# State-space layer and feed-forward on one core: where the sums over a chunk come from

## The chip, the cores and the metric

The kernel runs on one core of a Trainium2 chip. A core has five engines with queues of their own: TensorE (PE; its weight loads are listed as PEld), VectorE (DVE), ScalarE (ACT), GpSimd (POOL) and SyncE (SP), which here issues DMA transfers. The metric is the device time of one execution in microseconds; a comparison uses the median of several runs.

## The reference

For 16 sequences of 512 tokens with 256 channels, x goes through two blocks with a residual each. The first is a state-space layer (8 heads of 64, state size 128); the second a feed-forward layer with ternary weights. What matters here is the scan of the first:

```
dt = softplus(dt + dt_bias);  A = -exp(A_log)
dA = exp(dt * A)                      # per token and head
S  = dA_t * S + xdt_t B_t             # state, token after token
y_t = S C_t
```

With a = dt * A, a product of dA over a range of tokens is the exponential of a sum of a over that range.

## The kernel before

A sequence is cut into NC = 4 chunks of P = 128 tokens, and the scan is done chunk by chunk with matrix products. For each sequence and each of its 32 pairs (chunk, head), W = NC * NH, the kernel needs four things made of sums of `a`:

- the running sum at each token, as rows (`cum`, 32 x 128) and, transposed, as columns (`cums`, 128 x 32);
- the rows broadcast to all 128 partitions: `cum` is written to DRAM (`raw`, L464) and read back once for each chunk as `mt` (128 x 8 x 128, `stage_r`, L518). Then `relu(cums - mt)` is taken head by head (`stage_s`, L545, ScalarE; for the first sequence's chunks 1 to 3 `stage_s_v`, L532, VectorE), and an exponential over the tile (`stage_b1`, L556): the decay between two tokens of a chunk;
- `ecum`, the exponential of the rows (L485), broadcast through DRAM as `ct` (L495) and multiplied on POOL (L506);
- `dec` (L480): the exponential of two sums, the one over the tokens after each token of its chunk (`dec[:, 0]`) and the one over the whole chunk (`dec[:, 1]`). POOL uses the first in `xend` (L610), which feeds the product `pst` (L630) that updates the state, and the second to decay the state (L658).

`sums_of` makes all of them with products on TensorE: `after` and `ones` times `a` (L456) for the two sums of `dec`, copied by VectorE to `sums` (L462); `a` times `incl` (L457) for the rows, copied by ScalarE to `cum` (L461); and a transpose of `cum` (L468), copied to `cums` (L470). An f32 product of two operands is two passes on TensorE, each with its weight load.

Around this stand, for each sequence b: `stage_a` (projections `pm` L300 and `pz` L322, the causal convolution `cv` on ScalarE L305 and VectorE L307, silu L312 and L326, `dt` through `dtr` L339 and the transpose `pqt` L344), `stage_a2` (softplus, ends with `a`, L442), `stage_b2` (the chunks: transposes `px` L595, `pg` L601 and L602, `pst`, `py` L644 and L651, then `y` L663, `zs` L667, L574, L575), `stage_c1` (output projection `po` L716, norms, transposes of x3 and its split `x3p` L745 to L750) and `stage_c2` (feed-forward: `ph` L762, `hT` L768, `pf` L796). `stage_a0` and `stage_t0` give x (L259) and its transpose (`pt_a` L277, copied to `x1T` L280).

The order on each of the four compute engines is the order of issue in the program, which `interleave` makes: each stage is a generator with a sum of work and a place (from, to) between 0 and 1, and the stage whose next step has the smallest place goes on. After a prologue for sequences 0 and 1, the loop over i = 1 to 14 has two parts in a turn. The first part runs the projections of sequence i + 1 beside the output projection of i - 1; the second the chunks of i and the feed-forward of i - 1, beside the decays of i + 1. In the turn i = 1 the decays of sequence 1 are still done in the first part. Every wait is in order: an instruction that waits holds up all that is behind it on its engine.

Of the kernel before, what the change touches and what calls it, by code (L numbers as in the profile page):

```python
# [28 lines left out]
F32 = mybir.dt.float32  # L29
BF16 = mybir.dt.bfloat16  # L30
AF = mybir.ActivationFunctionType
ALU = mybir.AluOpType
# [3 lines left out]
P = 128  # L36
# [5 lines left out]
NH = 8  # L42
# [18 lines left out]
def mamba_ffn_kernel(  # L61
# [35 lines left out]
    def load_x(b):  # L97
# [12 lines left out]
    nc.gpsimd.affine_select(  # L110
        out=incl, in_=ones, compare_op=ALU.is_ge, fill=0.0, base=0,
        pattern=[[1, P]], channel_multiplier=-1,
    )
    after = const.tile([P, P], F32)
    nc.gpsimd.affine_select(
        out=after, in_=ones, compare_op=ALU.is_gt, fill=0.0, base=0,
        pattern=[[-1, P]], channel_multiplier=1,
    )
    mhalf = const.tile([P, NC], F32)
    nc.gpsimd.memset(mhalf, -0.5)  # L120
# [327 lines left out]
    def sums_of(b):  # L448


        W = NC * NH
        a = seqs[b].pop("a")
        af = a.rearrange("p c h -> p (c h)")
        pd = ps_tr.tile([P, 512], F32, tag="tr", name=f"pd_{b}")
        for i, tri in enumerate((after, ones)):
            nc.tensor.matmul(pd[:, i * W : (i + 1) * W], tri, af, start=True, stop=True)  # L456
        nc.tensor.matmul(pd[0:W, 2 * W : 2 * W + P], af, incl, start=True, stop=True)  # L457
        sums = small.tile([P, 2, W], F32, tag="sums", name=f"sums_{b}")
        pc = pd[0:W, 2 * W : 2 * W + P]
        cum = small.tile([W, P], F32, tag="cum", name=f"cum_{b}", bufs=1)  # L460
        nc.scalar.copy(cum, pc)  # L461
        nc.vector.tensor_copy(sums.rearrange("p i w -> p (i w)"), pd[:, 0 : 2 * W])  # L462
        raw = dram.tile([W, P], F32, tag="raw", name=f"raw_{b}")
        nc.sync.dma_start(raw, cum)  # L464
        seqs[b].update(sums=sums, cum=cum, raw=raw)
        yield 0.15
        turned = pd[:, 2 * W + P : 3 * W + P]
        nc.tensor.transpose(turned, cum, ident[0:W, 0:W])  # L468
        cums = small.tile([P, W], F32, tag="cums", name=f"cums_{b}", bufs=2)
        nc.vector.tensor_copy(cums, turned)  # L470
        seqs[b].update(cums=cums)
        yield 0.15


    def stage_b0(b):


        s = seqs[b]
        s["dec"] = small.tile([P, 2, NC, NH], F32, tag="dec", name=f"dec_{b}")
        nc.scalar.activation(  # L480
            s["dec"].rearrange("p i c h -> p (i c h)"), s["sums"].rearrange("p i w -> p (i w)"),
            AF.Exp,
        )
        ecum = small.tile([NC * NH, P], F32, tag="ecum", name=f"ecum_{b}", bufs=1)
        nc.scalar.activation(ecum, s.pop("cum"), AF.Exp)  # L485
        s["way"] = dram.tile([NC * NH, P], F32, tag="way", name=f"way_{b}")
        nc.sync.dma_start(s["way"], ecum)
        yield 0.1

    def stage_d(b):  # L490
# [35 lines left out]
    def stage_s_v(b, *chunks):  # L526

        s = seqs[b]
        for c in chunks:
            mt = s["mts"][c]  # L530
            for h in range(NH):
                nc.vector.tensor_scalar(  # L532
                    mt[:, h, :], mt[:, h, :], s["cums"][:, c * NH + h : c * NH + h + 1], 0.0,
                    ALU.subtract, ALU.min,
                )
                if h % 2 == 1:
                    yield 0.25

    def stage_s(b, *chunks):

        s = seqs[b]
        for c in chunks:
            mt = s["mts"][c]
            for h in range(NH):
                nc.scalar.activation(  # L545
                    mt[:, h, :], mt[:, h, :], AF.Relu,
                    bias=s["cums"][:, c * NH + h : c * NH + h + 1], scale=-1.0,
                )
                if h % 2 == 1:
                    yield 0.25  # L550
# [266 lines left out]
    def chain(*stages):  # L817
        for st in stages:
            yield from st
# [39 lines left out]
    with tc.manual_schedule(engines=ordered):  # L859
        interleave(  # L860
            (
                chain(stage_a0(0), stage_t0(0), stage_a(0, FIRST, 2)),
                A0_WORK + T0_WORK + A_WORK, 0.0, 1.0,
            ),
            (stage_a0(1), A0_WORK, 0.04, 0.28),
            (chain(stage_sil(0), stage_a2(0, False)), 0.8, 0.42, 0.64),
            (sums_of(0), 0.3, 0.78, 0.86),
            (stage_r(0, 0, 1, 2, 3), 0.4, 0.865, 0.88),
            (scales(1), 3.0, 0.55, 0.8),
        )  # L870
        run(stage_t0(1))
        run(stage_a6(0))
        interleave(
            (stage_a(1, SECOND, 2), A_WORK, 0.0, 0.8),
            (stage_s_v(0, 1, 2, 3), 3.0, 0.03, 0.18),
            (stage_s(0, 0), 1.0, 0.182, 0.184),
            (chain(stage_b0(0), stage_d(0), stage_b1(0, 0)), 0.3, 0.185, 0.187),
            (stage_b1(0, 1, 2, 3, sign=1.0), 0.3, 0.22, 0.225),
            (stage_b2(0), B2_WORK, 0.2, 0.88),
            (chain(stage_sil(1), stage_a2(1, False)), 0.8, 0.28, 0.44),  # L880
            (sums_of(1), 0.3, 0.5, 0.56),
            (ternary(1), 4.0, 0.52, 0.54),
            (stage_e(0), E_WORK, 0.27, 0.52),
            (scales(2), 3.0, 0.3, 0.6),
            (stage_r(1, 0), 0.1, 0.57, 0.571),
            (stage_r(1, 1), 0.1, 0.58, 0.581),
            (stage_a0(2), A0_WORK, 0.5, 0.75),
            (stage_s(1, 0), 1.0, 0.7, 0.74),
            (stage_s(1, 1), 1.0, 0.76, 0.79),
            (stage_r(1, 2), 0.1, 0.66, 0.661),  # L890
            (stage_r(1, 3), 0.1, 0.82, 0.821),
            (stage_t0(2), T0_WORK, 0.81, 0.83),
            (stage_a6(1), 0.1, 0.84, 0.841),
            (ternary(2, 0, 2), 2.0, 0.9, 0.91),
        )
        for i in range(1, NB - 1):
            interleave(
                (ending(), 0.1, 0.0, 0.01),
                *([(ternary(2, 2, 4), 2.0, 0.02, 0.08)] if i == 1 else []),
                *([(stage_a6(i), 0.1, 0.12, 0.13)] if i > 1 else []),  # L900
                (stage_a(i + 1, BESIDE, 2), A_WORK - 1.72, 0.0, 1.0),
                (
                    chain(
                        stage_b0(1), stage_d(1), stage_b1(1, 0, 1), stage_s(1, 2), stage_b1(1, 2),
                        stage_s(1, 3), stage_b1(1, 3),
                    ),
                    2.6, 0.015, 0.2,
                )
                if i == 1
                else (chain(stage_s(i, 3), stage_b1(i, 3)), 1.1, 0.0, 0.01),  # L910
                (stage_c1(i - 1), C1_WORK, 0.0, 1.0),
                (stage_e(i), E_WORK, 0.32, 1.0),
            )
            run(stage_a1(i + 1))
            second = [
                (stage_r(i + 1, 0, 1), 0.2, 0.365, 0.37),
                (stage_s(i + 1, 0), 1.0, 0.44, 0.49),
                (stage_b0(i + 1), 0.1, 0.5, 0.51),
                (stage_b1(i + 1, 0), 0.1, 0.515, 0.52),
                (stage_s(i + 1, 1), 1.0, 0.53, 0.61),  # L920
                (stage_b1(i + 1, 1), 0.1, 0.62, 0.63),
                (stage_r(i + 1, 2), 0.1, 0.63, 0.64),
                (stage_s(i + 1, 2), 1.0, 0.72, 0.8),
                (stage_b1(i + 1, 2), 0.1, 0.81, 0.82),
                (stage_r(i + 1, 3), 0.1, 0.82, 0.83),
            ]
            second.append((stage_c2(i - 1), C2_WORK, 0.02, 1.0))
            second.append((stage_b2(i), B2_WORK, 0.0, 0.98))
            second.append((stage_a2(i + 1), A2_WORK, 0.08, 0.36))
            second.append((stage_a5(i + 1), 1.7, 0.58, 0.66))  # L930
            second.append((stage_d(i + 1), 0.1, 0.92, 0.93))
            if i + 2 < NB:
                second.append((stage_a0(i + 2), A0_WORK, 0.6, 0.9))
                second.append((stage_t0(i + 2), T0_WORK, 0.94, 0.97))
            interleave(*second)
        run(stage_s(NB - 1, 3))
        run(stage_b1(NB - 1, 3))
        run(stage_a6(NB - 1))
        interleave(
            (ending(), 0.1, 0.0, 0.01),  # L940
            (stage_c1(NB - 2), C1_WORK, 0.0, 0.235),
            (stage_e(NB - 1), E_WORK, 0.03, 0.16),
            (stage_b2(NB - 1), B2_WORK, -0.02, 0.4),
            (stage_c2(NB - 2), C2_WORK, 0.235, 0.98),
            (stage_c1(NB - 1), C1_WORK, 0.42, 0.9),
        )
        interleave((ending(), 0.1, 0.05, 0.06), (stage_c2(NB - 1), C2_WORK, 0.0, 1.0))
# [43 lines left out]
```

## Time and profile before

| what | us |
|---|---|
| median of 3 runs | 1138.25 |
| the runs | 1136.69, 1138.25, 1140.64 |
| the profiled execution | 1138.89 |
| its span, first to last instruction | 1137.2 |
| one turn of the loop, `pst` of a sequence to that of the next | 67.20 |
| L456, four passes, on the chain that ended last | 0.37 |
| `dec` (L480), mean of 16 | 0.256 |
| sums copy (L462), mean of 16 | 0.218 |
| relu of one head (L545), mean of 488 | 0.388 |

How to read the profile: every engine's rows are of one execution. The busy share says how full an engine is, the chain of waits which work the end of the run waited for: it is followed back from the last instruction, at each step to what released it or to the instruction before it on its engine. In a timeline a row holds the start and the length in us, the engine, the line, the operation, `out<-in` with shapes and the count of merged instructions; in brackets the idle time before it and what ended it. Successive instructions of an engine may overlap at their ends.

### The profile page before, as it was taken

What the parts mean: (1) busy time and instruction counts of PE and PEld (TensorE: products, weight loads), DVE (VectorE), ACT (ScalarE), POOL (GpSimd) and SP (SyncE); (2) the same over time, 40 slices, a digit from 0 to 9 for tenths busy, and PEclk for the clock granted to TensorE, in tenths of its full rate; (3) what the DMA queues carried; (4) which work ended last, traced back from release to release, by engine and by line L of the source; (5) the groups of instructions that cost most, each with busy time, mean ns of one, the idle gap of its engine ahead of it and who ended that gap; (6) DMA issues with size and microseconds to landing.
All of it is one profiled execution on the core that took longest, in us unless ns stands there. A gap on an engine that the chain in (4) does not pass through costs nothing.

```text
span 1137.2 us, 17164 instructions
## 1 busy us (share of the span) xinstructions
PE 1076.8 (95%) x6052; PEld 708.8 (62%) x6052; DVE 826.9 (73%) x2141; ACT 696.4 (61%) x1378; POOL 581.9 (51%) x695
## 2 busy tenths in 40 slices
PE   5777999999999999999999999999999999999797
PEld 2334475665757567575766757576574756657575
DVE  4797859677695867769686786967778596776552
ACT  4738667566756665676666567666666675665421
POOL 1243646355464635646464565635446463556742
PEclk9998999999999999999999999999999999999899
DMA  5221130221203121220311212022120302212000
GB/s 200 107 97 59 32 128 28 77 93 57 95 20 134 34 76 75 76 94 19 124 46 57 94 56 103 29 90 79 57 94 27 133 29 76 74 57 94 1 10 28
DMA packets 34534, 81.23 MB, mean 71 GB/s; under 512 B 4368, under 2 KB 23440, under 8 KB 32400
## 3 DMA queue, kind: packets, MB, share of 16 engines
q1 hardware_dynamic: 32896, 79.97, 20.3%
q8 instruction: 48, 0.79, 0.3%
q10 hardware_dynamic: 1552, 0.16, 0.1%
q14 instruction: 38, 0.31, 0.1%
HBM read 71.21 MB, written 8.91 MB: 70 GB/s over the span
## 4 chain that ended last, share of the span: by engine, by line
PE 56%; POOL 17%; DVE 16%; ACT 8%; issue 2%; DMA 1%; POOLq 0%; ACTq 0%; DVEq 0%
PE pf L796 19%; PE ph L762 12%; POOL ct L506 9%; PE pm L300 6%; PE py L644 5%; ACT mt L545 4%; PE pst L630 4%; DVE cv L307 4%; PE py L651 3%; POOL x3p L750 3%; DVE st_f L228 2%; DVE x L702 2%; ACT cv L305 2%; ACT mt L556 1%; POOL xend L610 1%
## 5 line engine op out<-in xcount | busy, mean ns | idle before, releaser
L307 DVE SCALAR_TENSOR_TENSOR cv<-pm,cw_sb,cv 128x511 f32<-128x511 f32 (+2 forms) x288 | 215.3, 748 | 62.7 <-ACT cv L305 55.5
L796 PE MATMUL pf<-w_sb,hT 128*128 128x256 f32 x1024 | 238.0, 382 | 0.0
L796 PEld LDWEIGHTS pf<-w_sb,hT 128*128 128x128 f32 x1024 | 190.0, 190 | 35.8 <-issue 11.5
L762 PE MATMUL ph<-x3p,w_bf 128*128 128x512 bf16 x768 | 188.7, 380 | 4.3 <-POOL x3p L750 1.9
L300 PE MATMUL pm<-x1T,win_sb 128*128 128x512 f32 x384 | 186.5, 609 | 1.2 <-ACT state L633 0.9
L768 ACT ACTIVATE hT<-ph,b_sb 128x512 f32<-128x512 f32 x128 | 87.9, 688 | 130.1 <-PE ph L762 129.9
L545 ACT ACTIVATE mt<-mt,cums 128x128 f32<-128x128 f32 x488 | 152.3, 388 | 0.0
L667 POOL TENSOR_TENSOR zs<-y,zs 128x512 f32<-128x512 f32 x64 | 81.3, 1271 | 105.8 <-DVE y L663 104.2
L716 PE MATMUL po<-wo_sb,zs 128*128 128x256 f32 x512 | 123.5, 385 | 2.2 <-DVE att L722 2.1
L322 PE MATMUL pz<-x1T,win_sb 128*128 128x512 f32 x256 | 121.7, 598 | 3.7 <-DVE sp_a L431 3.7
L762 PEld LDWEIGHTS <-w_bf 128*128 128x128 bf16 x768 | 70.3, 98 | 87.9 <-issue 22.7
L300 PEld LDWEIGHTS pm<-x1T,win_sb 128*128 128x128 f32 x384 | 71.5, 194 | 72.5 <-issue 65.1
L506 POOL TENSOR_TENSOR ct<-ct,xbc 128x1024 f32<-128x1024 f32 x48 | 112.3, 2365 | 3.7 <-DMA ct<-way 3.7
L716 PEld LDWEIGHTS po<-wo_sb,zs 128*128 128x128 f32 x512 | 94.9, 190 | 29.9 <-issue 14.4
L305 ACT ACTIVATE cv<-pm,cw_sb 128x512 f32<-128x512 f32 x96 | 65.0, 677 | 70.4 <-PE pm L300 68.9
L575 POOL TENSOR_TENSOR y<-y 128x256 f32<-128x256 f32 x64 | 46.9, 733 | 115.6 <-ACT y L574 115.6
L663 DVE SCALAR_TENSOR_TENSOR y<-xbc,dsk,py 128x128 f32<-128x128 f32 x256 | 71.3, 341 | 44.2 <-PE py L651 39.7
L644 PE MATMUL py<-mt,xdt 128*64 128x128 f32 x1024 | 94.6, 279 | 1.5 <-ACT mt L556 0.8
L326 ACT ACTIVATE zs<-pz 128x512 f32<-128x512 f32 x64 | 37.9, 592 | 81.6 <-PE pz L322 81.5
L235 POOL TENSOR_TENSOR rs_c<-rs_c,mhalf 128x2 f32<-128x2 f32 x32 | 25.1, 784 | 119.6 <-DVE rms L586 88.7
L322 PEld LDWEIGHTS pz<-x1T,win_sb 128*128 128x128 f32 x256 | 47.7, 192 | 59.0 <-issue 51.2
L613 DVE TENSOR_TENSOR mt<-mt,pg 128x1024 f32<-128x1024 f32 x64 | 77.6, 1213 | 1.5 <-ACT mt L556 1.0
(131 smaller groups left out, 1794.5 us busy)
## 6 DMA issues: line engine op xcount, KB each, us to landing
mt<-raw SPq DMA_DIRECT2D x64, 512.0 KB, 3.9
ct<-way SPq DMA_DIRECT2D x16, 1536.0 KB, 6.3
xin<-in_x SPq DMA_DIRECT2D x16, 512.0 KB, 3.8
out<-o SPq DMA_DIRECT2D x30, 256.0 KB, 2.1
w_in<-in_w SPq DMA_DIRECT2D x1, 1024.0 KB, 8.7
w_sb<-in_w SPq DMA_DIRECT2D x1, 1024.0 KB, 10.9
win_sb<-in_w_in SPq DMA_DIRECT2D x1, 768.0 KB, 5.8
win_sb<-in_w_in SPq DMA_DIRECT2D x1, 512.0 KB, 8.3
```

The costliest lines, as they stand in the source:

```text
L300: nc.tensor.matmul(pm, win_sb[:, k, DI + m * P : DI + (m + 1) * P], x1T[:, k, :], start=(k == 0), stop=(k == 1),)
L305: nc.scalar.activation(cv, pm, AF.Copy, scale=cw_sb[:, m, 3:4])
L307: nc.vector.scalar_tensor_tensor(cv[:, j:], pm[:, 0 : L - j], cw_sb[:, m, 3 - j : 4 - j], cv[:, j:], ALU.mult, ALU.add,)
L322: nc.tensor.matmul(pz, win_sb[:, k, j * P : (j + 1) * P], x1T[:, k, :], start=(k == 0), stop=(k == 1),)
L506: nc.gpsimd.tensor_tensor(ct[:, c - 1], ct[:, c - 1], xbc[:, 5, c * P : (c + 1) * P].unsqueeze(1).to_broadcast([P, NH, P]), ALU.mult,)
L545: nc.scalar.activation(mt[:, h, :], mt[:, h, :], AF.Relu, bias=s["cums"][:, c * NH + h : c * NH + h + 1], scale=-1.0,)
L644: nc.tensor.matmul(py[h % 2 * HD : (h % 2 + 1) * HD, j, :], xdt[:, h * HD : (h + 1) * HD], mts[c][:, h, :], start=True, stop=(c == 0),)
L667: nc.gpsimd.tensor_tensor(zs[:, :, tok], y, zs[:, :, tok], ALU.mult)
L716: nc.tensor.matmul(po[:, 0:DM], g[:, k, c * P : (c + 1) * P], wo_sb[:, k, :], start=(k == 0), stop=(k == NJ - 1),)
L762: nc.tensor.matmul(ph, w1_bf[:, k, f * P : (f + 1) * P], x3p[:, j, k, :], start=(j == 0 and k == 0), stop=(j == 2 and k == 1),)
L768: nc.scalar.activation(hT[:, f, :], ph, AF.Gelu, bias=b1_sb[:, f : f + 1])
L796: nc.tensor.matmul(pf[:, 0:DM], hT[:, f, c * P : (c + 1) * P], w2_sb[:, f, :], start=(f == 0), stop=(f == NF - 1),)
```

## The change

The two sums of `dec` are no longer products. The sum over a chunk is the last running sum of the chunk, and this stands, already broadcast to all partitions, in the last column of `mt` before the relu overwrites it. So a new step `total` copies that column (128 x 8, every 128th element) to `sums[:, 1]` before the first relu of chunks 0, 1 and 2: by ScalarE in `stage_s`, by VectorE in `stage_s_v`. A new `stage_b3` subtracts `cums` on VectorE, which gives the sums after each token, and takes the exponential of both (128 x 48; chunk 3, which nobody uses, is left out). `stage_b3` stands ahead of chunk 2's exponential: in the loop at 0.805 to 0.81 of a turn's second part, in the turn i = 1 in the chain of sequence 1's decays, and for sequence 0 after `stage_d`. `stage_b0` keeps only `ecum` and its transfer. The constant `after`, the two products and VectorE's copy go.

```diff
-        for i, tri in enumerate((after, ones)):
-            nc.tensor.matmul(pd[:, i * W : (i + 1) * W], tri, af, start=True, stop=True)
-        nc.tensor.matmul(pd[0:W, 2 * W : 2 * W + P], af, incl, start=True, stop=True)
+        nc.tensor.matmul(pd[0:W, 0:P], af, incl, start=True, stop=True)
...
-        nc.vector.tensor_copy(sums.rearrange("p i w -> p (i w)"), pd[:, 0 : 2 * W])
...
     def stage_b0(b):
-        s["dec"] = small.tile([P, 2, NC, NH], F32, tag="dec", name=f"dec_{b}")
-        nc.scalar.activation(
-            s["dec"].rearrange("p i c h -> p (i c h)"), s["sums"].rearrange("p i w -> p (i w)"),
-            AF.Exp,
-        )
...
+    def total(b, c, copy):
+        if c < NC - 1:
+            copy(seqs[b]["sums"][:, 1, c, :], seqs[b]["mts"][c][:, :, P - 1])
+
+    def stage_b3(b):
+        s = seqs[b]
+        sums = s["sums"]
+        nc.vector.tensor_sub(
+            sums[:, 0], sums[:, 1],
+            s["cums"][:, 0 : (NC - 1) * NH].rearrange("p (c h) -> p c h", h=NH),
+        )
+        s["dec"] = small.tile([P, 2, NC - 1, NH], F32, tag="dec", name=f"dec_{b}")
+        nc.scalar.activation(s["dec"], sums, AF.Exp)
+        yield 0.1
...
     def stage_s_v(b, *chunks):
+            total(b, c, nc.vector.tensor_copy)
...
     def stage_s(b, *chunks):
+            total(b, c, nc.scalar.copy)
...
-            (chain(stage_b0(0), stage_d(0), stage_b1(0, 0)), 0.3, 0.185, 0.187),
+            (chain(stage_b0(0), stage_d(0), stage_b3(0), stage_b1(0, 0)), 0.4, 0.185, 0.187),
...
-                        stage_b0(1), stage_d(1), stage_b1(1, 0, 1), stage_s(1, 2), stage_b1(1, 2),
-                        stage_s(1, 3), stage_b1(1, 3),
+                        stage_b0(1), stage_d(1), stage_b1(1, 0, 1), stage_s(1, 2), stage_b3(1),
+                        stage_b1(1, 2), stage_s(1, 3), stage_b1(1, 3),
...
+                (stage_b3(i + 1), 0.1, 0.805, 0.81),
                 (stage_b1(i + 1, 2), 0.1, 0.81, 0.82),
```

More of the change, by code (lines that the diff above doesn't have):

```diff
@@ L112, in mamba_ffn_kernel @@
         pattern=[[1, P]], channel_multiplier=-1,
-    )
[L114 to L117, printed above, removed]
     )
@@ L454, in sums_of @@
         pd = ps_tr.tile([P, 512], F32, tag="tr", name=f"pd_{b}")
-        for i, tri in enumerate((after, ones)):
[L456 to L459, printed above, removed]
+        nc.tensor.matmul(pd[0:W, 0:P], af, incl, start=True, stop=True)
+        sums = small.tile([P, 2, NC - 1, NH], F32, tag="sums", name=f"sums_{b}")
+        pc = pd[0:W, 0:P]
         cum = small.tile([W, P], F32, tag="cum", name=f"cum_{b}", bufs=1)
         nc.scalar.copy(cum, pc)
-        nc.vector.tensor_copy(sums.rearrange("p i w -> p (i w)"), pd[:, 0 : 2 * W])
         raw = dram.tile([W, P], F32, tag="raw", name=f"raw_{b}")
@@ L466, in sums_of @@
         yield 0.15
-        turned = pd[:, 2 * W + P : 3 * W + P]
+        turned = pd[:, P : W + P]
         nc.tensor.transpose(turned, cum, ident[0:W, 0:W])
@@ L478, in stage_b0 @@
         s = seqs[b]
-        s["dec"] = small.tile([P, 2, NC, NH], F32, tag="dec", name=f"dec_{b}")
-        nc.scalar.activation(
-            s["dec"].rearrange("p i c h -> p (i c h)"), s["sums"].rearrange("p i w -> p (i w)"),
-            AF.Exp,
-        )
         ecum = small.tile([NC * NH, P], F32, tag="ecum", name=f"ecum_{b}", bufs=1)
@@ L903, in mamba_ffn_kernel @@
                     chain(
-                        stage_b0(1), stage_d(1), stage_b1(1, 0, 1), stage_s(1, 2), stage_b1(1, 2),
-                        stage_s(1, 3), stage_b1(1, 3),
+                        stage_b0(1), stage_d(1), stage_b1(1, 0, 1), stage_s(1, 2), stage_b3(1),
+                        stage_b1(1, 2), stage_s(1, 3), stage_b1(1, 3),
                     ),
-                    2.6, 0.015, 0.2,
+                    2.7, 0.015, 0.2,
                 )
```

## The prediction

> **What bounds the kernel now.** The page's busy rows come first, to see which engine is full; then its line on the chain that ended last, to see whether a full engine is also a late one.
>
> ```profile
> PE 1076.8 (95%) x6052; PEld 708.8 (62%) x6052; DVE 826.9 (73%) x2141; ACT 696.4 (61%) x1378; POOL 581.9 (51%) x695
> ...
> PE 56%; POOL 17%; DVE 16%; ACT 8%; issue 2%; DMA 1%; POOLq 0%; ACTq 0%; DVEq 0%
> ```
>
> PE is busy 95% of the span, but only 56% of the chain is PE: the rest passes through POOL, DVE and ACT while PE does work that is not late. So I read the chain in order of time for one turn of the steady loop (440 to 520 us; columns: start, duration, what).
>
> ```profile
> 466.17 1.13 PE pst L630 x2
> ...
> 473.51 0.37 PE pd L456 x4
> 473.88 0.34 PE pd L457 x2
> ...
> 504.14 1.84 PE pm L300 x4
> 505.98 0.02 issue
> 506.00 0.69 ACT cv L305
> ```
>
> From 466.17 to 505.98 the chain is PE alone, piece against piece; from 506.00 to the next turn's pst at 533.37 it goes through ACT, DVE and POOL. A turn is 67.20 us. The two removed products (L456, four passes) lie in the PE part, with 0.37 us. There are 14 turns, so this is the steady prize. The first 130 us are another matter: there the chain changes engine all the time, and I read them from the timelines of each engine, beside the order in which the two kernels, as built, put instructions on each engine.
>
> **The steady turn: what goes.** Start to start, PE's timeline gives L602 at 473.24, L456 at 473.35, L457 at 473.81, second L457 at 473.94, next ph at 474.15. If L457 took L456's place outright, 473.81 - 473.35 = 0.46 us would go. But L457 uses 32 columns of the array where its neighbours use 128, and after such a change of shape the next weight load starts late: the last L457 to ph takes 0.20, where 128-column neighbours of that size are 0.11 apart. Hence L457 can load at 473.24 + 0.20 = 473.44, and 0.37 goes, as the chain says. I take 0.365; the ends are 0.36 and 0.46. TensorE waits for `a` (DVE L442, ends 473.08) and that is 0.36 before the earliest load, so no new wait. 14 x 0.365 = **5.1 us**.
>
> The Trainium skill (TensorEngine Tiling (Array Packing), Key Properties) says that a change of tiling mode drains TensorE; the 0.20 us agrees. Without that rule the term would be 14 x 0.46 = 6.4 us.
>
> The transpose L468 has to wait for DVE's sums copy (0.76 us idle weight-load time in the turn), but it starts 0.52 after the pst before it, a 512-wide pass (0.43) plus the same shape change, so I give nothing for the dropped wait there.
>
> **The steady turn: what comes.** Three ScalarE copies of 128x8, one before the relus of chunks 0, 1 and 2. No row shows such a copy. The nearest are an activation of 128x8 (209 ns, L165) and one of 128x32 (213 ns, L393); a copy that read the whole 128x1024 tile would be like L556, 1048 ns. Bounds 0 and 1.05; I take 0.20, since 8 elements are read, though 512 bytes apart. The first relu then waits for the copy on its own engine, because it overwrites what the copy read. Independent ScalarE instructions overlap by 0.10, dependent ones start 0.02 after (L556 after L545), so a copy costs 0.10 + 0.10 + 0.02 = 0.22 us of ScalarE. The exponential `dec` leaves its place beside ecum (0.16) and returns before chunk 2's.
>
> ScalarE is delayed by 2 x 0.22 - 0.16 = 0.28 us when it reaches cv (489.30), and DVE, POOL and the zs of chunk 2 after it. What covers that: ScalarE idles 2.98 us before y at 495.79 for POOL; the four x (done 499.55) are wanted by PE only at 501.84; and here, with `dec` added too:
>
> ```profile
> 502.31 1.07 ACT L280 COPY x1T<-pt_a 128x512 f32<-128x512 f32 x2 [0.78 <-PE pt_a L277]
> 506.00 0.69 ACT L305 ACTIVATE cv<-pm,cw_sb 128x512 f32<-128x512 f32 x1 [2.62 <-PE pm L300]
> ```
>
> Ahead of the x1T copies stands y of chunk 3 (from 500.90, after 0.41 idle), so they could begin at 501.43 + 0.28, against 502.31: 0.6 us is left, and pm behind them has another 0.6. The subtraction on DVE (like L442, 0.19) falls into DVE's 1.20 us idle before 499.29; `dec` comes after the x, at 499.5, so it does not wait for DVE. The copies take over the DMA wait of the first relu, which had none. SP issues the same transfers in the same order. Chunk 3 has no copy, so the ACT part of the chain at 506 is unchanged. Cost: 0, with the cover named; without it, at most the 0.28.
>
> **The first sequence.** Here L468's wait does count; chain, 25 to 90 us:
>
> ```profile
> 35.78 0.14 DVE sums L462
> 35.92 0.04 issue
> 35.97 0.25 PE pd L468
> 36.21 1.91 PE pm L300 x4
> ```
>
> The sums copy sat in DVE's queue behind three cv steps. Without it L468 waits only for cum on ScalarE, free at 34.83: copy to 34.99, L468 at 35.03, **0.93 earlier**, and PE carries the chain to 47.2. Then one copy on ScalarE ahead of the relus that are on the chain: +0.22. `dec` moves behind ecum and waits for DVE's two copies and subtraction (50.76 + 2 x 0.17 + 0.19 = 51.29), which ends before ecum does; nothing more. The sums copy of sequence 1 on the chain at 75.26: -0.13. Sum -0.84; bounds -1.1 to 0, since DVE and POOL slow each other around 60 and 75 us.
>
> **The first turn (i = 1).** Here the moved exponential meets a new wait. ScalarE's order becomes cv, `dec`, exp of chunk 2, eight relus, exp, dtr. `dec` needs the subtraction, and that stands on DVE behind the three steps that consume this very cv:
>
> ```profile
> 106.88 0.66 ACT L305 ACTIVATE cv<-pm,cw_sb 128x512 f32<-128x512 f32 x1
> 107.45 1.04 ACT L556 ACTIVATE mt<-mt 128x1024 f32<-128x1024 f32 x1
> ...
> 111.82 0.25 ACT L339 COPY dtr<-pq 128x128 f32<-128x128 f32 x1
> ```
> ```profile
> 107.58 2.32 DVE L307 SCALAR_TENSOR_TENSOR cv<-pm,cw_sb,cv 128x511 f32<-128x511 f32 x3 [0.81 <-ACT cv L305]
> 109.81 0.48 DVE L722 SCALAR_TENSOR_TENSOR att<-po,rms,x 128x256 f32<-128x256 f32 x1
> ```
>
> The subtraction ends at 109.81 + 0.19, `dec` starts at 110.05, the exponential at 110.25 instead of 107.45: 2.8 us. Before that ScalarE has taken three copies less `dec`'s old place, 0.66 - 0.16 = 0.50, on the chain (89.65 to 106.97 is ScalarE's work or waits on it). So dtr is 3.3 us late. Queued behind it is PE: the transpose pqt (L344, 112.17) stands in order before 18 us of projections with no idle time until 129.58; then pst starts at 130.21. The late PE delays zs and the casts of x3p on ScalarE (125.88 + 3.3), POOL's x3p starts at 129.75 instead of 126.91 and xend behind it ends 2.9 later. Cost **+2.9**; bounds 2.6 (3.3 less PE's 0.63 idle) and 3.3.
>
> **Sum.** -5.1 - 0.84 + 2.9 = -3.1 us. The profiled execution took 1138.89 us (span 1137.2, 1.7 around it): 1135.8. It lies 0.6 above the median of the runs, 1138.25; from that the same sum gives 1135.2.
>
> **Rivals.** *The clock drops in the new wait.* PE will idle about 2.4 us before pqt, after 2.09 before po. The stretches show what such an idle can do (PEclk is the column after POOL):
>
> ```profile
> 72.50:76.00 3.50, 0.79 (x6) 0.66 (x7) 3.36 (x11) 0.21 (x1) 3.50 (x3) 0.99 0.25 81
> 76.00:79.40 3.40, 3.40 (x9) 1.90 (x8) 3.33 (x5) 0.00 (x0) 3.02 (x2) 0.51 0.96 349
> ```
>
> After 2.71 us idle (72.73 to 75.44) the granted clock was 0.51 for 3.4 us. Against it: 3.75 us idle at 60.41 did not do so. Half speed for 3.4 us costs 1.7: 1137.5. The Trainium skill (TensorE: Matmul & The Clock Gate, Part 1) wants an idle window of about 3.4 us; by that rule there is no drop, but the 2.71 us here contradict a strict reading.
>
> *The stall is hidden*: if PE and ScalarE catch up before pst, the 2.9 shrinks to about 1, and it is 1133.9. For it: ScalarE idles 0.84 and 1.12 around 114 to 116. Against: PE has none.
>
> *The removal does not reach the end*: another chain holds the turn at 67.20, and only the first 130 us change, +2.0: 1140.9. Against it, 40 us of chain without a gap in PE; for it, POOL and DVE carry the next 27.
>
> *Dear copies (slower).* If a copy's 512-byte steps make it as slow as L556, 1.07 of ScalarE each: delay at cv 1.98, x1T starts 1.1 late, less pm's 0.6 leaves 0.48 a turn against 0.365 gained, and four copies at the start cost 3.4 more: 1138.89 + 14 x 0.12 + 2.0 + 3.4 = 1146. It decides from 0.85 us a copy on. Only the unknown stride speaks for it.
>
> **Chances.** Forecast 0.50; clock 0.18; hidden stall 0.12; no gain 0.12; dear copies 0.08. Range 1132.5 to 1140.5: it leaves out the dear copies and the far half of no gain. 0.3% is 3.4 us, about what a measurement of this kernel can tell from no change; the forecast lies just inside. Faster: 0.20 of the forecast, the hidden stall and a little of the clock, 0.34. Slower: dear copies and a little, 0.10. The same: 0.56.
>
> **What would show it.** Turns of 66.83 us between the pst of two sequences; L602 to L457 0.20; 128x8 copies of 0.2 us; no wait of PE for x1T. L468 right behind cum near 35.0. In the first turn a ScalarE wait for DVE of about 2.5 us ahead of `dec`, PE waiting for dtr, pst near 132.2. The prediction is wrong if turns stay at 67.2, or if copies cost several times 0.2.

## The result, and the profile after

The changed kernel takes 1135.94 us (median of 20 runs, 1134.13 to 1139.61), the kernel before 1138.02 (20 runs, 1135.85 to 1141.03): ratio 0.9983, 95% interval [0.9976, 0.9990], some 2 us less. A second set (after_again, below) gave 1135.95 against 1138.67, 0.9976 [0.9967, 0.9985]. The forecast was 1135.8 us, 3.1 less than before. The profiled execution took 1138.18 (span 1136.5), which is 2.2 above its kernel's median; where it lost time is found below.

First the page of the changed kernel, the busy rows and the line of the chain that ended last:

```profile
PE 1080.3 (95%) x5988; PEld 704.3 (62%) x5988; DVE 831.5 (73%) x2143; ACT 705.3 (62%) x1424; POOL 581.6 (51%) x694
...
PE 57%; POOL 16%; DVE 14%; ACT 9%; issue 2%; DMA 1%; SPq 0%; ACTq 0%; POOLq 0%
```

TensorE has 64 instructions fewer (16 sequences, four passes each), yet is busy 3.5 us longer than before. Fewer passes and more busy time mean slower passes: once it had come up, the granted clock was at half speed for 43.7 us of this execution, and for 25.6 of the one before. Then a steady turn, in the chain of the changed kernel (start, duration, what):

```profile
468.81 1.12 PE pst L635 x2
...
475.82 0.22 PE pg L606 x2
476.15 0.34 PE pd L450 x2
476.49 1.40 PE ph L767 x6
...
506.41 1.84 PE pm L295 x4
508.27 0.69 ACT cv L300
```

The row of the two sums is gone, and from pst to pm it is 37.60 us, before 37.97 (504.14 - 466.17). The 13 full turns are 66.80 to 66.83 us, forecast 66.83; the last step, from pst of sequence 14 to that of 15, is 41.62 for 41.97. The first sequence, same chain:

```profile
35.35 0.14 ACT cum L454
...
35.54 0.25 PE pd L460
```

The transpose stands right behind `cum`; DVE's `sums` is out of its way. And the first turn:

```profile
109.74 0.75 DVE cv L302
110.49 0.10 DVE sums L485
...
110.61 0.24 ACT dec L490
...
115.43 0.47 PE pqt L339
115.91 3.09 PE pz L317 x4
119.00 1.72 PE pm L295 x4
...
134.73 1.13 PE pst L635 x2
```

This is the new wait: `dec` on ScalarE stands behind the subtraction, and that behind the last convolution step on VectorE. But pst comes at 134.73, not at 132.2, and one row shows why: four passes of pz take 3.09, and the same four passes of pm behind them 1.72.

Starts of whole executions differ, so I measure from one landmark to the next: from the product `ttot` (in the prologue, ahead of everything changed) to pst of sequence 0, from there to `dtr` of the first turn, and from `dtr` to pst of sequence 1.

| profile | ttot to pst 0 | pst 0 to dtr | dtr to pst 1 | pst 0 to pst 1 | turn |
|---|---|---|---|---|---|
| before | 20.92 | 58.91 | 18.39 | 77.30 | 67.20 |
| after | 20.39 | 62.23 | 19.60 | 81.83 | 66.82 |
| after_again | 20.40 | 62.44 | 18.07 | 80.51 | 66.82 |
| e1_early_sub | 20.40 | 59.42 | 18.26 | 77.68 | 66.83 |
| e2_no_products | 19.97 | 58.21 | 18.40 | 76.61 | 66.83 |
| e3_products_kept | 20.62 | 62.36 | 18.44 | 80.80 | 67.21 |
| e4_wide_copies | 21.33 | 64.26 | 20.58 | 84.84 | 68.00 |
| e5_full_shape | 20.31 | 62.37 | 19.77 | 82.14 | 66.45 |
| e6_shape_and_early | 20.31 | 59.71 | 19.62 | 79.33 | 66.43 |
| e7_three_more_copies | 20.71 | 62.36 | 18.46 | 80.82 | 66.82 |
| e8_fill_before_pss | 20.40 | 63.90 | 19.77 | 83.68 | 66.83 |
| e9_fill_before_pqt | 20.40 | 62.48 | 18.88 | 81.36 | 66.82 |
| e10_all | 20.30 | 60.02 | 18.25 | 78.27 | 66.43 |
| e11_fill_five | 20.39 | 59.03 | 18.49 | 77.52 | 66.82 |

Between pst 0 and `dtr` executions differ by more than most edits. The first x on ScalarE in this stretch (L254, before L259) starts 53.7 to 54.3 us behind `ttot` in after, after_again, e1, e8 and e9, but 52.9 in e11, and all six are the same program up to there. The largest part is a meeting of VectorE and POOL, here in after_again and then in e11:

```profile
57.33 2.25 DVE L421 TENSOR_TENSOR sp_z<-sp_z,sp_s 128x32 f32<-128x32 f32 x1
57.18 2.35 POOL L509 TENSOR_TENSOR ct<-ct,xbc 128x1024 f32<-128x1024 f32 x1 [3.67 <-DMA ct<-way]
```
```profile
56.44 0.19 DVE L421 TENSOR_TENSOR sp_z<-sp_z,sp_s 128x32 f32<-128x32 f32 x1
56.47 2.37 POOL L509 TENSOR_TENSOR ct<-ct,xbc 128x1024 f32<-128x1024 f32 x1 [3.85 <-DMA ct<-way]
```

If POOL's product has begun when L421 comes, L421 takes 2.2 to 2.4 us and the operation behind it (L423) 0.96; if L421 comes just ahead of it, it takes 0.19 and L423 takes 2.2 to 2.3. The first happened in nine profiles, the second in five (e2, e4, e7, e10, e11), which gain some 0.8 us by it: from the start of L421 to y on VectorE (L668, in e11 L674) it takes 3.17 us in after_again and 2.37 in e11. So one pair of profiles does not price an edit in this stretch to better than about a microsecond; short distances between two rows do.

### The profile page after: what moved, and what is told of

It reads as the page before. It is cut to its first block, busy times and chain, and to the rows that moved or that the text cites. A ratio compares the mean times of both kernels' runs of the same rounds, so it can differ in the third digit from the quotient of the medians.

```text
span 1136.5 us, 17062 instructions
## 1 busy us (share of the span) xinstructions
PE 1080.3 (95%) x5988; PEld 704.3 (62%) x5988; DVE 831.5 (73%) x2143; ACT 705.3 (62%) x1424; POOL 581.6 (51%) x694
## 4 chain that ended last, share of the span: by engine, by line
PE 57%; POOL 16%; DVE 14%; ACT 9%; issue 2%; DMA 1%; SPq 0%; ACTq 0%; POOLq 0%
PE pf L801 19%; PE ph L767 12%; POOL ct L509 8%; PE pm L295 6%; PE py L649 5%; ACT mt L550 4%; PE pst L635 4%; DVE cv L302 3%; PE py L656 3%; POOL x3p L755 3%; DVE st_f L223 2%; DVE x L707 2%; PE pz L317 2%; ACT mt L561 2%; ACT cv L300 2%
## 5 line engine op out<-in xcount | busy, mean ns | idle before, releaser
L295 PE MATMUL pm<-x1T,win_sb 128*128 128x512 f32 x384 | 189.5, 617 | 0.3 <-ACT x1T L275 0.3
L668 DVE SCALAR_TENSOR_TENSOR y<-xbc,dsk,py 128x128 f32<-128x128 f32 x256 | 71.3, 340 | 44.0 <-PE py L656 40.6
L649 PE MATMUL py<-mt,xdt 128*64 128x128 f32 x1024 | 95.5, 281 | 1.1 <-ACT zs L321 0.7
```

The lines of the kernel that those rows point to most:

```text
L295: nc.tensor.matmul(pm, win_sb[:, k, DI + m * P : DI + (m + 1) * P], x1T[:, k, :], start=(k == 0), stop=(k == 1),)
L649: nc.tensor.matmul(py[h % 2 * HD : (h % 2 + 1) * HD, j, :], xdt[:, h * HD : (h + 1) * HD], mts[c][:, h, :], start=True, stop=(c == 0),)
```

## The experiments

The theory: the turns give 5.2 us, the new wait of the first turn takes some 3 back, and the clock of TensorE takes a further part of it in some executions. Rivals: the copies on ScalarE cost in every turn; the loss at the start is no matter of the wait.

**The wait alone.** In e1_early_sub only sequence 1's subtraction moves, to right behind the third copy on VectorE, ahead of the convolution's three steps:

```diff
+            if b == 1 and c == 2:        # in stage_s, behind total()
+                after_tokens(b)          # the tensor_sub of stage_b3
...
+        if b != 1:                       # in stage_b3
+            after_tokens(b)
```

> The changed kernel with one instruction moved on one engine, in the turn i = 1 only: VectorE's subtraction is issued right behind the third copy of the column, so that it no longer stands behind the three cv steps that wait for ScalarE. Theory A (the first turn loses to dec's wait for the subtraction, 2.8 us): ScalarE reaches dec without a wait, dtr comes about 2.8 us earlier against the copies, the first pst of sequence 1 comes near 130 to 131 us instead of 134.7, turns stay at 66.82, and the time is 3 to 4 us under the changed kernel's, about 1132.5. Theory B (the three copies on ScalarE are what costs): pst of sequence 1 stays within 0.5 us and the time at 1136. Theory C (only the clock's drop differs from run to run): the median stays at 1136.

Measured: 1135.5 us (1131.96 to 1139.19), ratio 0.9969 [0.9958, 0.9981]; the expectation was about 1132.5. ScalarE in the changed kernel, and here:

```profile
107.47 0.67 ACT L300 ACTIVATE cv<-pm,cw_sb 128x512 f32<-128x512 f32 x1
110.61 0.24 ACT L490 ACTIVATE dec<-sums 128x48 f32<-128x48 f32 x1 [2.48 <-DVE sums L485]
110.76 1.04 ACT L561 ACTIVATE mt<-mt 128x1024 f32<-128x1024 f32 x1
```
```profile
106.62 0.66 ACT L300 ACTIVATE cv<-pm,cw_sb 128x512 f32<-128x512 f32 x1
107.19 0.23 ACT L496 ACTIVATE dec<-sums 128x48 f32<-128x48 f32 x1
107.32 1.04 ACT L569 ACTIVATE mt<-mt 128x1024 f32<-128x1024 f32 x1
```

From cv to the exponential it is 3.29 us in all nine profiles with the late subtraction and 0.70 in all three with the early one: the wait costs **2.59 us** on ScalarE. From landmark to landmark it looks like more: pst 0 to dtr falls from 62.44 (after_again) to 59.42, pst 0 to pst 1 from 80.51 to 77.68, 2.83, forecast 2.9. Of this, 0.4 is won ahead of cv (75.18 and 74.75 behind `ttot`) and 0.2 lost again behind `dtr`. The copies show between two rows of ScalarE: at the x above e1 is 0.65 ahead of the kernel before, at this cv 0.14, so the three copies less the old place of `dec` cost 0.51, forecast 0.50. But the median fell by only 0.8 to 1.6 us against the two sets of the changed kernel (0.9969 for 0.9976 and 0.9983). In its profile the span, 1132.8, is only 0.15 under that of after_again: the 2.83 are won, 1.50 are lost ahead of `ttot` and 1.05 behind pst of sequence 14, at each place with a stretch of 3.4 us at half clock (at 17.5 and 1038.1) that after_again doesn't have. Whether the other executions lost it in the same way has no profile.

**The removal alone.** In e2_no_products `dec` is the exponential of `cums`, taken twice, where it was before; the two sums are left out of the computation, and there are no copies and no subtraction.

```diff
-        for i, tri in enumerate((after, ones)):
-            nc.tensor.matmul(pd[:, i * W : (i + 1) * W], tri, af, start=True, stop=True)
...
+            s["cums"].unsqueeze(1).to_broadcast([P, 2, NC * NH]), AF.Exp,
```

> The kernel before with only the removal: the two products and VectorE's copy of the sums are gone, dec is the exponential of cums taken twice at its old place, so the two sums are left out of the computation; no copies, no subtraction, dec not moved. Theory A (steady gain is TensorE's 0.37 us a turn, the new copies are covered): turns of 66.82 to 66.83 as in the changed kernel, the first pst of sequence 1 near 129.3 us and 1132 us in all. Theory B (the copies cost something in every turn): turns shorter than 66.8, and 0.2 us a turn is 3 us more of gain, 1129. If the products were not on the path, turns stay at 67.19.

Measured: 1134.72 us (1132.29 to 1136.15), ratio 0.9960 [0.9945, 0.9976], turns of 66.83 as in the changed kernel. So the three copies and the subtraction cost a steady turn nothing. At the start they do: ttot to pst 0 is 19.97 here and 20.40 with them. The time is 2.7 above the expected 1132: against after_again its profile loses 3.1 us ahead of `ttot` and 1.0 behind pst of sequence 14, with half clock from 17.0 and from 1037.6 on. That pst 0 to dtr is 0.7 shorter than before fits the early L421 above (0.8), and need not be the removal.

**The other half.** e3_products_kept is the changed kernel with the two products still issued and unread.

```diff
+        for i, tri in enumerate((after, ones)):
+            nc.tensor.matmul(
+                pd[:, 2 * P + i * W : 2 * P + (i + 1) * W], tri, af, start=True, stop=True
+            )
```

> The changed kernel with the two products still issued on TensorE, their results unread: the copies, the subtraction and the moved exponential alone. Theory A: turns of 67.19 as before, since the copies hide; the start keeps its loss, so the time is the kernel before plus 2 to 4 us, about 1141. Theory B (copies cost in every turn): turns of 67.3 or more. If the start lost nothing by the wait for VectorE, the time is that of the kernel before, 1138.

Measured: 1144.36 us (1139.52 to 1146.2), ratio 1.0040 [1.0026, 1.0055]. Turns are 67.21 again and pst 0 to pst 1 80.80 as in after_again. The expectation was about 1141. With the changed kernel at -2 to -3 us, the products are worth some 7 to 8 us of medians. Its profile is 8.7 us longer than after_again: 5.4 in the turns, 1.7 ahead of `ttot` and 1.1 behind pst of sequence 14, both with a stretch at half clock (at 19.0 and 1046) that after_again doesn't have, and 0.5 between `ttot` and pst 1. So the trace shows 5.4 for the turns, 0.2 ahead of pst 0, and for most of the rest the clock; whether the medians are made up in the same way stays open.

**The shape.** In e5_full_shape `a` lies in a zeroed 128x128 tile, so that the rows and their transpose are 128x128 products like their neighbours.

```diff
-        nc.tensor.matmul(pd[0:W, 0:P], af, incl, start=True, stop=True)
+        nc.tensor.matmul(pd[:, 0:P], a, incl, start=True, stop=True)   # a: 128x128, zeroed
...
-        nc.tensor.transpose(turned, cum, ident[0:W, 0:W])
+        nc.tensor.transpose(pd[:, P : 2 * P], rows, ident)
```

> The changed kernel with the row sums and the transpose of cum made as 128 x 128 products (columns 32 to 127 of the operand are zeros), so that TensorE never changes the shape of its tile here. Theory A (the 0.20 and 0.52 us around these products are the wait after a change of shape): the row sums follow pg at 0.11 and ph follows 0.22 later, 0.21 us a turn saved; the transpose follows pst at 0.43, 0.16 saved; turns of 66.45 and 1131 us. Rival (those gaps are something else, such as the wait for cum or for a): turns of 66.8 to 66.9, the time 1136 to 1137, since the transpose streams 128 columns instead of 32.

Measured: 1131.12 us (1129.69 to 1133.03), ratio 0.9932 [0.9916, 0.9947], turns 66.45. TensorE's timeline (start, length, operation) in a steady turn of the changed kernel, and of this one:

```profile
475.88 0.27 PE L607 MATMUL pg<-ident,xbc 128*128 128x128 f32 x1
476.08 0.41 PE L450 MATMUL pd<-incl,a 128*32 128x128 f32 x2
476.42 0.82 PE L767 MATMUL ph<-x3p,w_bf 128*128 128x512 bf16 x3
```
```profile
472.12 0.27 PE L611 MATMUL pg<-ident,xbc 128*128 128x128 f32 x1
472.23 0.39 PE L453 MATMUL pd<-incl,a_wide 128*128 128x128 f32 x2
472.46 1.46 PE L771 MATMUL ph<-x3p,w_bf 128*128 128x512 bf16 x5
```

From pg's last pass to ph it is 0.54 us with 128x32 weights and 0.34 with 128x128 ones; pg to pd alone 0.20 and 0.11, as the prediction had read the shape change. The transpose gives the rest of the 0.37 (from pst's start to the ph behind it 1.13 us with 32x32, timeline of e2_no_products, and 0.97 here). The products are larger and the turn is shorter: what a small product costs on the chain is not its columns. That it is the change, and not a narrow shape by itself, shows in single passes that no edit touched: in the same turn of the changed kernel ph (128x128) to px (128x128) is 0.22 us from start to start, ph to py (128x64) 0.31, and py to ph 0.20, where one pair of py follows the other after 0.10. Each change costs about 0.10.

**Both edits.** e6_shape_and_early joins e5 and e1.

> The changed kernel with both single edits: row sums and transpose as 128x128 products, and the subtraction of sequence 1 issued on VectorE right behind the third copy. If the two effects are independent: pst of sequence 1 near 130 (132.8 with the shape alone, 129.95 with the early subtraction alone), turns of 66.45 us, and 1128.0 to 1130.5 us against 1131.1 with the shape alone. Rival (clock windows): the clock at half speed sets the start, the early subtraction brings nothing beside the full shape, and it is 1131 again.

Measured: **1129.24 us** (1125.96 to 1130.11), ratio 0.9906 [0.9892, 0.9921]. pst 0 to pst 1 is 79.33 against 82.14 in e5: 2.81, the wait a second time. It beats both kernels.

**The copies' price.** e4_wide_copies has a copy of the whole tile beside each small one, e7_three_more_copies three more small ones.

```diff
             total(b, c, nc.scalar.copy)
+            if c < NC - 1:
+                nc.scalar.copy(spare, mt)                          # e4
...
+                for i in range(3):
+                    nc.scalar.copy(spare[:, i], mt[:, :, P - 1])   # e7
```

> The changed kernel with one more ScalarE copy beside each small one, of the whole 128x1024 tile into a spare one that nothing reads (about 1.05 us each): the price at which the prediction's rival of dear copies was to decide. By the prediction's slack (x1T 0.6, pm 0.6) ScalarE reaches cv 2.1 us later than in the changed kernel, 2.4 later than in the kernel before, and each turn is 0.5 to 0.95 late: turns of 67.3 to 67.8, and with 3.4 to 4.3 at the start 1146 to 1155 us. If ScalarE's waits hide more than the prediction counted, turns stay at 66.83 and only the start pays: 1139 to 1141.

> The changed kernel with three more 128x8 copies of the same column beside each small one, into a spare tile that nothing reads. Independent copies of about 0.19 us that overlap by 0.10: 0.3 us more at each place, 0.6 at cv. If the prediction's cover (0.6 at x1T, 0.6 at pm) is right, turns stay at 66.82 to 66.84 and the start is 1.0 to 1.5 later: 1137 to 1138.5 us. If the changed kernel has no cover left, each turn is 0.6 longer, 67.4, and the time 1145.

Measured: e4 1159.69 us (1159.16 to 1160.85), ratio 1.0187 [1.0173, 1.0201], turns 68.00; e7 1139.45 (1137.07 to 1140.41), ratio 1.0005 [0.9996, 1.0014], turns 66.82. In e4 the chain of a turn leaves TensorE for ScalarE and comes back through the copy of x:

```profile
492.11 0.95 ACT spare L551
...
513.91 0.48 ACT x1T L276
514.44 0.83 PE pss L590 x6
515.27 1.84 PE pm L296 x4
```

pm comes 38.79 us behind pst, 1.19 later than in the changed kernel, and cv on ScalarE 1.89 later (24.98 behind pst against 23.09). So the cover is 0.70, not the 0.6 + 0.6 that was counted: x1T starts 1.57 later, and from x1T to pm it is 1.45 for 1.83. Ahead of x1T the idle time of 0.45 is used up, but y of chunk 3, which waits for POOL's zs, comes 2.1 later, more than cv. Behind x1T 0.38 is there and no more, since the six passes of pss stand between x1T and pm in TensorE's order. The range expected for e4 was too low, by 0.2 a turn and by 5 us in all. e7 stays inside this cover. Its median is 1 us above the expectation; the turns do not hold it, and its profile loses 2.8 us ahead of `ttot` against after_again.

**The clock.** In the changed kernel's profile the granted clock is 0.5 in 53.69 to 60.52, 74.17 to 81.00, 94.65 to 101.48 and 111.71 to 118.54. The lengths are multiples of 3.41 us, in every profile, and so are the distances; only the last stretch, at the end of the execution, is cut. So I laid a grid of 3.41 us through each profile's clock steps and summed up TensorE's busy time per cell. The windows of the kernel before at the idle time that the prediction used as evidence against a drop (stretch, length, then busy us of PE, PEld, DVE, ACT and POOL, then the granted clock):

```profile
58.88:62.29 3.41, 1.53 (x9) 0.70 (x6) 3.31 (x5) 2.49 (x4) 2.71 (x2) 1.00 0.00 0
62.30:65.71 3.41, 1.55 (x4) 0.68 (x4) 3.34 (x9) 0.32 (x1) 1.90 (x2) 1.00 0.00 0
```

The 3.75 us idle from 60.41 fell half into one cell and half into the next, and both stayed busy 45%: no drop. The idle time of 2.07 us ahead of po in the changed kernel's first turn fell whole into one:

```profile
108.30:111.71 3.41, 1.34 (x8) 1.15 (x7) 3.23 (x8) 1.09 (x2) 0.00 (x0) 1.00 0.47 192
111.71:115.12 3.41, 2.47 (x7) 1.40 (x5) 2.00 (x7) 3.38 (x10) 1.39 (x3) 0.50 0.00 0
```

Busy 39%, and the next cell is at half clock. Over all 14 profiles (from 18 to 140 us, and from 1030 us to some 14 us before the end), of the cells at full clock: busy under 40%, 57, all of them followed by half clock; 40 to 60%, 57, of which 9 were; over 60%, 607, none.

> The changed kernel once more, for a second profile of its start. If the 2.5 us by which pst of sequence 1 came later than forecast (134.73 against 132.2) is the clock falling to half speed around 111.7, it hangs on where the idle times fall against the clock's steps, and this profile shows pst between 132 and 135, later by about half of the time spent at half speed behind pqt. If it is a wait of the change itself, pst stands at 134.7 again with the clock at full speed there.

Measured: after_again has the clock at full speed from 98.4 to 1057.5. Its idle times ahead of po and pqt, 2.27 and 2.41 us, fall into cells that are 47, 58 and 57% busy. dtr to pst is 18.07 there and 19.60 in the first profile: the drop cost 1.5 us of that execution. The rest of the wait is as in the first profile (62.44 and 62.23). The first profile's span is 3.5 longer: 2.1 ahead of `ttot`, where it was at half clock from 19.6 to 23.0, and 1.3 between pst 0 and pst 1.

To show cause and not only company, TensorE was given products that nothing reads, in the 5.6 us that it idles ahead of pss; behind this idle time the clock went to half, at 90.6 to 95.5 us, in all eleven profiles that have it unfilled.

```diff
+            if b == 0 and lo == 0:
+                fill = ps_c.tile([P, L], F32, tag="c", name="fill")
+                for _ in range(11):                       # e8, e10; e11: 5
+                    nc.tensor.matmul(
+                        fill, win_sb[:, 0, 0:P], win_sb[:, 0, 0:L], start=True, stop=True
+                    )
```

> The changed kernel with 11 products of 128x512 (0.43 us each, 4.7 us), whose result nothing reads, put on TensorE ahead of the first sum of squares of sequence 0, in the 5.6 us in which it idles there before pss. In all profiles so far the clock is at half speed behind this idle time (from 91 to 101 us), and in them a stretch of 3.41 us of the clock's own grid in which TensorE is busy under 0.40 is followed by one at half speed. By this rule no drop follows here any more, pss and pm behind it take 2.6 us instead of 4.8, and pst of sequence 1 comes 77.5 to 79.0 us behind pst of sequence 0 (80.5 to 81.8 in the changed kernel): about 2 us less, 1133 to 1134.5. Rival: the clock falls for another reason (load, a fixed pattern at the start), is at half speed around 95 again, and the time stays at 1136 or rises by what the products delay.

> Full-shape products, the early subtraction and the 11 products before pss together: the version of the single results. If the clock's part adds to the others, 2 us below the 1129.2 of the first two: 1126.5 to 1128; if it doesn't, 1129 again. Turns 66.43, pst of sequence 1 at 75 to 77 us behind pst of sequence 0.

Measured: e8 1137.98 us (1136.91 to 1141.0), ratio 1.0001 [0.9992, 1.0009]; e10 1129.75 (1127.41 to 1132.38), ratio 0.9928 [0.9912, 0.9943]. In both the drop there is gone. The gain isn't there, since I had mis-sized the products: an f32 product is two passes, so eleven took 9.61 us and held pss back. With five:

> The changed kernel with 5 instead of 11 products of 128x512 ahead of pss. The eleven ran 9.61 us (22 passes of 0.43, two to a product), not the 4.7 of the expectation, and held pss back by 3 to 4 us; the clock stayed at full speed behind them. Five are 4.4 us and fit into the 5.6 us. If the idle time is what takes the clock down, it is at full speed from 88 to 105 again, pss and pm take 2.6 us instead of 4.8, pst of sequence 1 comes 78.5 to 80.0 us behind pst of sequence 0 where no other drop follows (80.5 in the changed kernel), and the median is 1 to 2 us under the changed kernel's, 1134 to 1135. Rival: the drop at 91 to 95 returns, and nothing is gained.

Measured: 1133.72 us (1130.87 to 1134.85), ratio 0.9955 [0.9943, 0.9967]. TensorE's timeline in after_again, without the products:

```profile
94.08 1.44 PE L587 MATMUL pss<-ones,sq 128*128 128x1 f32 x6 [5.60 <-ACT x1T L275]
95.37 3.46 PE L295 MATMUL pm<-x1T,win_sb 128*128 128x512 f32 x4
```

and in e11 with them:

```profile
91.87 0.83 PE L593 MATMUL pss<-ones,sq 128*128 128x1 f32 x6 [1.31 <-ACT x1T L275]
92.56 1.96 PE L295 MATMUL pm<-x1T,win_sb 128*128 128x512 f32 x4
```

The same work takes 2.49 us instead of 4.59 (to the po behind it). pst 0 to pst 1 is 77.52, 3.0 less, but 1.3 of this was won ahead of the products, by the x above. Products that compute nothing make the kernel 2 us faster: the idle time is the cause of the drop. (In e11 another fell at 105.0, behind 2.05 us idle ahead of po.)

**A filled new wait.** e9_fill_before_pqt puts four such products ahead of pqt, in the wait of the change.

```diff
             pq = ps_a.tile([P, L], F32, tag="a", name=f"pqt_{b}")
+            if b == 2:
+                for _ in range(4):
+                    nc.tensor.matmul(
+                        pq, win_sb[:, 0, 0:P], x1T[:, 0, :], start=True, stop=True
+                    )
```

> The changed kernel with 4 products of 128x512 (1.7 us), whose result nothing reads, on TensorE ahead of the transpose pqt of the first turn, in the 1.25 to 2.4 us in which it waits there for dtr. By the rule of the clock's stretches only the idle time before po (2.1 to 2.5 us) is left to take the clock down around 111; dtr to pst stays 18.0 to 18.5 unless that one falls into one stretch. If the new idle time costs the medians something, 1135.2 to 1135.9; if the products delay pqt, 1136 to 1137. The steps of the sum (turn 66.83, dtr late by 3.3) are as in the changed kernel.

Measured: 1138.16 us (1134.86 to 1142.68), ratio 1.0004 [0.9990, 1.0017]. Sized by the same mistake, they took 3.60 us and pqt came 0.9 later than `dtr` allowed; no drop followed. The median is 1 us above the range that was expected for late products. What the second idle time alone costs the medians stays open.

## Why the prediction was right, and where not

The time fell 0.1 us from the forecast, and the mechanisms are the ones named; what the first 130 us cost was summed too low.

- **Turns.** Right: 66.82 to 66.83 against 66.83; the removed passes lie on the chain, the copies (185 to 195 ns, forecast 200) are covered. That a shape change and not the columns set the price is shown by e5. The Trainium skill's rule (TensorEngine Tiling (Array Packing), Key Properties), a drain at each change of tiling mode, agrees with it: e5 keeps one shape and saves another 0.37 us a turn.
- **First sequence.** The transpose: from ttot 3.98 before, 3.03 after, 0.95 earlier; forecast 0.93. The first exponential on ScalarE, through which the chain runs on, starts 51.83 - 31.99 = 19.84 behind ttot before and 51.63 - 32.51 = 19.12 after, 0.72 earlier: the 0.93 less 0.22 for the copy, as forecast. But pst gains only 20.92 - 20.39 = 0.53. The step that failed is "dec moves behind ecum ...; nothing more". POOL's `xend`, which pst waits for, starts when `dec` ends, before and after:

```profile
51.81 1.04 POOL L610 TENSOR_TENSOR xend<-xdt,dec 128x512 f32<-128x512 f32 x1 [9.67 <-ACT dec L480]
```
```profile
51.80 1.04 POOL L615 TENSOR_TENSOR xend<-xdt,dec 128x512 f32<-128x512 f32 x1 [9.14 <-ACT dec L490]
```

  `dec` was the first behind the relus and now stands behind ecum, so xend and pst 0 lose 0.2 more. The rows behind pst do not show the loss: the copy of the state on ScalarE (L638, before L633), which reads pst, is 0.72 earlier too.
- **First turn.** The wait: right. cv to exponential is 3.29 for 0.57, 2.72 more, forecast 2.8. From ttot `dtr` comes 2.8 later than before in the first profile and 3.0 in after_again, forecast 3.3 - 0.84 = 2.5. pst 1 comes 4.0 and 2.7 later, forecast 2.9 - 0.84 = 2.1. Of the 0.6 too much in after_again, 0.5 stands already at the x named under the table, where only 0.25 is left of the 0.72: in the stretch in which executions differ. The -0.13 of the sums copy at 75 us can't be seen.
- **The sum.** The turns give 5.2, so after_again comes to -5.2 + 2.7 = -2.5 for -3.1; the first profile has 1.3 more in the first turn. The medians, -2.1 and -2.7, lie near.
- **The clock.** The rival had 0.18 and stood as an alternative to the forecast. It was both: with the late subtraction a drop came between po's idle time and pst of sequence 1 in 7 of 9 profiles, without it in 1 of 5 (e6), and where it reached beyond dtr by more than 2 us (first profile, e5, e6, e8; e4 has wide copies there too) it cost 1.2 to 1.7. It should have been a term, not a case. Of the seven, five came from po's idle time (2.05 to 3.2 us), which the kernel before has too (2.09) and which in its profile was split by the grid, and two (e5, e8) from the new one ahead of pqt. So the new wait gives the clock a second place to fall at; how often it does, 14 profiles can't say. The reason against it, "3.75 us idle at 60.41 did not do so", was chance of the grid. The Trainium skill (TensorE: Matmul & The Clock Gate, Part 1) has free-running windows of 3413 ns, and the grid here agrees; that the clock falls only after an idle window doesn't: 39% busy is enough, in every case.
- **Dear copies.** Rightly unlikely; but the cover behind them was overrated (0.70 for 1.2), so they would have decided from a lower price than 0.85 us. That the forecast hit the median to 0.1 is in part luck: its reference execution, 1138.89, is 0.9 above before's median of 20 runs.

## What to carry to other kernels

A result that is needed early must not be queued, on an in-order engine, behind work that only later steps need: one small subtraction behind three convolution steps took back about half of what 14 turns had gained, and issuing it earlier cost nothing that the rows show. Before small products are removed, see whether they can take their neighbours' shape: that was worth as much as the removal itself. Where TensorE has idle times of about 2 us, read the clock rows of more than one execution before a microsecond is put down to the program.

## What was not expected of the hardware

- TensorE's clock is decided on a fixed grid of 3.41 us: a cell busy under 40% (more than 2.0 us idle) halved the next in 57 of 57 cases, and the same idle time split over two cells doesn't. The grid's phase differs from execution to execution; `ttot` stands at 29.5 to 30.8 us without a drop ahead of it, at 31.8 to 32.5 with one of 3.4 us, at 33.5 with one of 6.8 (e2), and at 33.1 in e7, whose clock is first on record at full speed at 23.5 us, in the others at 13.6 to 16.5.
- Between 40 and 60% busy it can go either way: four cells at 1034 to 1043 us, 57 to 59% busy, were followed by half clock, and after_again's at 1037, 57% busy, wasn't. What tells these apart the runs don't show.
- A ScalarE copy of 128x8 elements 512 bytes apart takes 185 to 195 ns; the exponential of 128x8 elements without a stride takes 209. A copy of that size without a stride is in no run.
- A VectorE operation on 128x32 elements that takes 0.19 us alone takes 2.2 to 2.4 when a POOL product on 128x1024 (2.35) has begun beside it; in the case shown it ended 0.05 us behind that product.
